# A two-layer convolution-attention kernel: image 1's first normalisation is placed amid image 0's last tiles, and the last tiles' value products are split

## The chip, the cores and the metric

The kernel runs on one core of one Trainium2 chip. Its time is device microseconds (us) of that core; a time quoted for a kernel is the median of several executions. A profile is one execution taken by the hardware profiler. Its engines are PE (TensorE, matmul), PEld (its weight loads), DVE (VectorE), ACT (ScalarE), POOL (GpSimd) and SP (SyncE, here a queue that issues DMAs).

## The reference, cut to what matters

`x` holds 2 images of 256 channels and 64 x 64 places, in float32. Two layers follow each other, each added to its input:

```python
def _gn(v, G=32, eps=1e-5):            # group normalisation over groups of 8 channels
    g = v.reshape(B_, G, C_ // G, H_, W_)
    m = jnp.mean(g, axis=(2, 3, 4), keepdims=True)
    s = jnp.var(g, axis=(2, 3, 4), keepdims=True)
    return ((g - m) / jnp.sqrt(s + eps)).reshape(v.shape)

# layer 0: attention of 8 heads of 32 channels over all 4096 places
qkv = einsum('bchw,oc->bohw', _gn(x), qkv_w) + qkv_b
attn = softmax(einsum('bhci,bhcj->bhij', q, k) * scale)
x = x + einsum('bhij,bhcj->bhci', attn, v)
# layer 1, on _gn(x): attention of 64 places inside groups, twice (first over the
# "lr" grouping, then, on its result, over the "sr" grouping), and a convolution branch
qx = relu_bn(fq2, relu_bn(fq1, feats)); kx = relu_bn(fk2, relu_bn(fk1, feats))
vx = fv(feats)
feats2 = relu_bn(srW, softmax(qx.T kx * C**-0.5) applied to vx)
x = x + rate1 * feats2 + rate2 * conv3x3(...)
```

The normalisation of an image needs its whole image: mean and variance over eight channels and 4096 places.

## The kernel before, in words

**Stages.** The images are handled one after the other. An image has 8 tiles of 512 places (`NT` = 8, `T` = 512); a tile of x is 128 partitions by 2 channel halves by 512, 512 KB. For each image the stages are: statistics and normalisation of x for layer 0 (`Stats`, lines 295 to 340; `normalise`, 366); projections to queries, keys and values (`project0`, line 416, whose results go to DRAM by line 425); the long attention (`attention0`); the first part of layer 1 (`layer1_first`); and its second part (`layer1_second`), a loop over the 8 tiles `t`.

**A tile of the second part.** It runs the q branch (two products, `fq1` and `fq2`, each followed by a relu on ACT, lines 1349, 1358 and 1137), the k branch in the same way, and `group_attention`: the scores `sp` (line 1078), values `pvs` (line 1060, two halves of two groups, each group four products on PE), a softmax (`nm`, `e`, `den`, lines 1094 to 1101: DVE, with the exponential on ACT), transposes `at` (1106), copies of them into a block-diagonal tile `bd` on DVE (1115), the product `pc` of bd and values (1124), and a relu to `res` on ACT. In between stand 16 turns of the convolution (`conv_step`): `mm`, 32 products on PE (line 996), then `z`: a copy on ACT (1001) and four sums on DVE (1002 to 1005), then additions into x (1017 to 1023). `mm` has one buffer of four PSUM banks, so the next turn's products wait for the last sum. POOL makes the transformed input `v` of a turn from the padded normalised image `xp` (982, 986). When the turns of two tiles are done, `give` (1325) adds `res` to x and SP writes it out (1331).

**Image 1's beginning.** `following` is a generator that `layer1_second` advances in image 0's last tile. It issues the loads of image 1's x (line 70) and layer 0's weights on POOL (105, 109), 16 `bn_stats` (line 321), two aggregations (325), the mean over a group's channels as a product with the matrix `group8` (328), four small operations, the variance product (337), a square root on ACT (340) and a reciprocal (341). After the second part, the loop over images allocates `xn`, the normalised image, and normalises the 16 halves of tiles into it (366). `xn` takes the one large buffer that `xp` of image 0 held.

**What sets the order.** A planner puts instructions on each engine's queue by its own estimate of their times, so an instruction written late can stand early in its queue where its inputs allow. Inside `tc.manual_schedule(engines=...)` the engines named keep the written order; in the second part this is PE alone. `tc.issue_after(kept["given"])` keeps image 1's statistics behind the last `give`. Each engine's queue is worked off in order. x has nine tile buffers (`NT + 1`): tile 0 of image 1 is loaded at the kernel's start, and each further one when a tile of image 0 has been given. The tiles `w4` of the work pool have 12 buffers; PSUM in the second part is four banks for `mm` and four more (`bank`).

Of the kernel before, what the change touches and what calls it, by code (L numbers as in the profile page):

```python
# [9 lines left out]
F32 = mybir.dt.float32  # L10
# [7 lines left out]
P = 128  # L18
B, C, H, W = 2, 256, 64, 64
N = H * W  # L20
T = 512
# [19 lines left out]
def direct_layers(ctx: ExitStack, tc: tile.TileContext, a: dict, out: bass.AP, bad: bass.AP):  # L41
# [21 lines left out]
        return psum["ps"].tile(shape, F32, tag="bank", name=name)  # L63


    def load_x(b):
        tiles = []
        for t in range(NT):
            xt = xpool.tile([P, KC, T], F32, tag="x", name=f"x_{b}_{t}")
            nc.sync.dma_start(  # L70
                out=xt,
                in_=a["x"][b, :, t * T : (t + 1) * T].rearrange("(k p) n -> p k n", p=P),
            )
            tiles.append(xt)
        return tiles
# [910 lines left out]
            (nc.gpsimd.tensor_add if plus else nc.gpsimd.tensor_sub)(dst, rows(one), rows(two))  # L986
        return v

    def conv_step(b, xts, wf, v, s, q, pacc):


        mm = pacc.tile([P, 2, 4, STRIP], F32, tag="acc", name=f"mm_{b}_{s}_{q}")
        for r in range(4):
            for m in range(2):
                for k in range(KC):
                    nc.tensor.matmul(  # L996
                        mm[:, m, r, :], wf[:, k, 4 * r + q, m * P : (m + 1) * P], v[r // 2][:, r % 2, k, :],
                        start=k == 0, stop=k == KC - 1,
                    )
        z = w4([P, 2, 2, STRIP], f"z_{b}_{s}_{q}")  # L1000
        nc.scalar.copy(z[:, 1], mm[:, :, 1, :])  # L1001
        nc.vector.tensor_add(z[:, 0], z[:, 1], mm[:, :, 0, :])  # L1002
        nc.vector.tensor_add(z[:, 0], z[:, 0], mm[:, :, 2, :])
        nc.vector.tensor_sub(z[:, 1], z[:, 1], mm[:, :, 2, :])
        nc.vector.tensor_sub(z[:, 1], z[:, 1], mm[:, :, 3, :])  # L1005
        bias = kept["bias"][1]
        for half in range(2):
            xs = xts[2 * s + half].rearrange("p m (i r j c) -> p m i r j c", i=4, r=2, c=2)
            for r in range(2):
                zs = z[:, r, :, half * (STRIP // 2) : (half + 1) * (STRIP // 2)].rearrange(  # L1010
                    "p m (i j) -> p m i j", i=4
                )
                for c in range(2):
                    dst = xs[:, :, :, r, :, c]
                    if q - c == 0:
                        for m in range(2):
                            nc.vector.scalar_tensor_tensor(  # L1017
                                dst[:, m], zs[:, m], bias[:, m, 0:1], dst[:, m], ALU.add, ALU.add
                            )
# [24 lines left out]

    SC1 = C ** -0.5

    def group_attention(nm, q, k, tokens, wv, out, busy=False, apart=False, more=None, between=None):

# [2 lines left out]

        vs = w4([P, 4, C], f"vs_{nm}")

        def values(half):
            pv = bank([P, 2, C], f"pvs_{nm}_{half}")
            for i in range(2):
                for c in range(KC):
                    nc.tensor.matmul(  # L1060
                        pv[:, i, :], tokens(c, 2 * half + i), wv[:, c, :], start=c == 0, stop=c == KC - 1
                    )
            dst = vs[:, 2 * half : 2 * half + 2, :]
            if half == 0 or busy or apart:
                nc.scalar.copy(dst, pv)
            else:
                nc.vector.tensor_copy(dst, pv)
# [20 lines left out]
            yield  # L1088
        if not first:
            values(0)  # L1090
        if not apart:
            values(1)
        nm4 = small.tile([P, 4], F32, tag="nm4", name=f"nm4_{nm}")
        nc.vector.tensor_reduce(nm4, sp, AX.X, ALU.max, negate=True)
# [22 lines left out]
            )  # L1117
        if apart:
            values(1)
        yield  # L1120
        for m in range(KC):
            pc = bank([P, T], f"pc_{nm}_{m}")
            for w in range(4):
                nc.tensor.matmul(  # L1124
                    pc[:, w * P : (w + 1) * P], vs[:, w, m * P : (m + 1) * P],
                    bd[:, w].rearrange("p a i -> p (a i)"), start=True, stop=True,
                )
            out(m, pc)
            if m == 0 and between:
                between()  # L1130

    def product(pt, wt, src, m, last=True):
        for k in range(KC):
# [145 lines left out]
    def layer1_second(b, xts, feats, mean, rstd, shift, pacc, following):  # L1279
# [28 lines left out]
        }  # L1308
        images = {1: range(5), 3: (5, 6), 4: (7,)} if b == 0 else {0: (3, 4), 1: (5,), 2: (6,), 3: (7,)}

        def conv():
            nonlocal done, wf
            if wf is None:
                wf = fetch_conv_weights(b)
            if done + 1 < len(turns):
                ahead[done + 1] = conv_transform(b, xp, *turns[done + 1])
            conv_step(b, xts, wf, ahead.pop(done), *turns[done], pacc)
            done += 1

        def give(n):  # L1320
            res = results.pop(n)
            halves = out[b, :, n * T : (n + 1) * T].rearrange("(k p) n -> p k n", p=P)
            final = b == B - 1 and n == NT - 1
            for m in range(KC):
                kept["given"] = nc.vector.scalar_tensor_tensor(
                    res[:, m, :], res[:, m, :], wts["rate1"], xts[n][:, m, :], ALU.mult, ALU.add
                )
                if final:
                    (nc.scalar if m else nc.sync).dma_start(out=halves[:, m, :], in_=res[:, m, :])
            if not final:  # L1330
                nc.sync.dma_start(out=halves, in_=res)
# [7 lines left out]
        for t in range(NT):  # L1339
# [2 lines left out]
                feats[k][:, 8 * t : 8 * t + 8].rearrange("p o d e -> p (o d e)") for k in range(KC)  # L1342
            ]

            def branch(one, two, col1, col2, nm):
                hid = w4([P, KC, T], f"h{nm}_{nt}")
                ph = [bank([P, T], f"ph{nm}_{nt}_{m}") for m in range(KC)]
                for k, m in ((0, 0), (0, 1), (1, 0), (1, 1)) if t == 0 else ((0, 0), (1, 0), (0, 1), (1, 1)):
                    nc.tensor.matmul(  # L1349
                        ph[m], wts[one][:, k, m * P : (m + 1) * P], f[k], start=k == 0, stop=k == KC - 1  # L1350
                    )
                    if k == KC - 1:
                        bn_relu(hid[:, m, :], ph[m], col1, m)
                res = w4([P, KC, T], f"r{nm}_{nt}")
                pr = [bank([P, T], f"pr{nm}_{nt}_{m}") for m in range(KC)]
                for k in range(KC):
# [5 lines left out]
                    bn_relu(res[:, m, :], pr[m], col2, m)  # L1362
                return res

            with tc.manual_schedule(engines={mybir.EngineType.PE}):
                q = branch("fq1", "fq2", V_FQ1, V_FQ2, "q")
                if pending:
                    next(pending)
# [2 lines left out]
                for tt in images.get(t, ()):  # L1371
                    to_image(tt)
                if 0 in spots.get(t, ()) and (b or t > 2):
                    conv()
                if b == 0 and t == NT - 1:
                    for n in sorted(results):
                        give(n)
                k = branch("fk1", "fk2", V_FK1, V_FK2, "k")
                if b == 0 and t == 2:
                    conv()  # L1380
                res = w4([P, KC, T], f"res_{nt}")
# [1 line left out]
                def to_res(m, pc, res=res):  # L1383
# [5 lines left out]

                parts = group_attention(  # L1390
                    nt, q, k, lambda c, w, f=f: f[c][:, w * P : (w + 1) * P], wts["fv"], to_res, apart=t + 1 < NT,
                    between=lambda: next(then) if b == 0 and t == NT - 1 else None,
                )
                next(parts)
                if 1 in spots.get(t, ()):
                    conv()
                if t < 2 and b == 0:
                    pending = parts
                else:
                    next(parts)  # L1400
                    if b == 0 and t == NT - 1:
                        next(then)
                    next(parts, None)
                    if b == 0 and t == NT - 1:
                        next(then)
                if 2 in spots.get(t, ()):
                    conv()
            if b == 0 and t == 1:
# [12 lines left out]
            results[t] = res  # L1421
            for n in sorted(n for n in results if done >= 4 * (n // 2 + 1)):
                give(n)


    ahead = {}

    def following():

        ahead.update(xts=load_x(1), w0=load_layer0(1))  # L1430
        with tc.issue_after(kept["given"].ins):
            steps = group_stats(ahead["xts"], "l0_1")
            next(steps)
        yield
        next(steps)
        yield
        ahead["stats"] = next(steps)
        yield

    for b in range(B):  # L1440
        xts = x_first if b == 0 else ahead["xts"]
        w0 = w0_first if b == 0 else ahead["w0"]
        with tc.tile_pool(name=f"ps0_{b}", bufs=8, space=PSUM) as psum["ps"]:
            mean, rstd = list(group_stats(xts, "l0_0"))[-1] if b == 0 else ahead["stats"]
            xn = apool.tile([P, KC, N], F32, tag="A", name=f"xn_{b}")
            for t in range(NT):
                for k in range(KC):
                    normalised = normalise(xn[:, k, t * T : (t + 1) * T], xts[t][:, k, :], k, mean, rstd)
# [574 lines left out]
```

## Time and profile before

| | us |
|---|---|
| median of 3 executions | 3069.78 (3066.59 to 3073.84) |
| profiled execution | 3067.66 |
| its span, first to last instruction | 3065.9 |
| mean granted clock of PE | 0.993 of full |

| stretch of the span | what runs there |
|---|---|
| 1320 to 1533 | image 0's second part, tiles 2 to 7, with the 16 convolution turns |
| 1533 to 1552 | end of tile 7, statistics of image 1 |
| 1552 to 1639 | image 1's normalisation and projections |
| 3047 to 3058 | the last tile of image 1 |

In a line of the timeline the first number is the start, the second the duration, in us from the span's start; then engine, line, operation, output and input, shapes and how many were merged; in brackets the idle time before it and what ended it. A line of the list of waits reads: who, waiting for whom: us in total, how often, longest. A table of stretches gives busy us of each engine, the granted clock of PE (1.00 is full), the mean busy share of the 16 DMA engines and the GB/s that they moved.

### The profile page before, as it was taken

To read this page: it belongs to the slowest core of one execution; us is meant where nothing else is said; L and a number is where in the kernel's file an instruction comes from. 1 tells how busy PE (TensorE), PEld (TensorE's weight loads), DVE (VectorE), ACT (ScalarE), POOL (GpSimd) and SP (SyncE) were. 2 spreads that over 40 slices of the span, in tenths; PEclk is the share of its full clock that TensorE was granted. 3 is DMA by queue.
4 is the path that set the end of the run, shared out by engine and by line. 5 is a ranking of instruction groups with operands and counts; after the bars stand their busy time and mean duration, and the time that the engine had idled before them with its cause. 6 is when DMAs were issued, how large, how long until landed. Compare 5 with 4: busy or idle time off the path is not lost. (4 is left out here: it accounts for less than half of the span.)

```text
span 3065.9 us, 63941 instructions
## 1 busy us (share of the span) xinstructions
PE 2986.3 (97%) x25129; PEld 1863.2 (61%) x25129; DVE 2456.4 (80%) x3122; ACT 2340.4 (76%) x3266; POOL 832.6 (27%) x918
## 2 busy tenths in 40 slices
PE   7999999999999999999989999999999999999998
PEld 4565566665556556677755655566555565576765
DVE  4698998989899999856556989989989999835543
ACT  2699999999999983622227999999999999734333
POOL 1122222222223240155301222322222222306440
PEclk9999999999999999999999999999999999999999
DMA  7968789787897661220159688797788976700000
GB/s 259 278 133 179 153 161 177 152 167 161 172 185 160 141 135 32 86 118 28 45 195 271 129 177 163 159 182 145 172 166 170 183 147 128 169 4 4 21 15 22
DMA packets 244148, 425.01 MB, mean 139 GB/s; under 512 B 98888, under 2 KB 109948, under 8 KB 241660
## 3 DMA queue, kind: packets, MB, share of 16 engines
q0 software_dynamic: 94720, 237.57, 40.1%
q1 hardware_dynamic: 148972, 182.99, 21.6%
q8 instruction: 199, 3.26, 0.4%
q14 instruction: 113, 0.93, 0.1%
q10 hardware_dynamic: 144, 0.26, 0.0%
HBM read 119.55 MB, written 68.39 MB: 61 GB/s over the span
## 5 line engine op out<-in xcount | busy, mean ns | idle before, releaser
L551 ACT ACTIVATE es<-ring 128x512 f32<-128x512 f32 (+2 forms) x1572 | 1203.4, 904 | 29.6 <-PE ring L545 21.7
L545 PE MATMUL ring<-q,k 128*128 128x512 f32 x4096 | 1082.3, 407 | 10.1 <-ACT v L551 4.8
L597 DVE TENSOR_TENSOR e<-e,es 128x1024 f32<-128x1024 f32 (+1 forms) x956 | 1035.3, 1144 | 23.1 <-ACT es L551 22.6
L545 PEld LDWEIGHTS ring<-q,k 128*128 128x128 f32 x4096 | 733.7, 188 | 379.8 <-ACT es L551 114.5
L551 ACT ACTIVATE v<-ring 128x512 f32<-128x512 f32 (+2 forms) x1024 | 780.7, 899 | 23.7 <-PE ring L545 12.8
L560 PE MATMUL av<-es,v 128*32 128x256 f32 (+1 forms) x9684 | 725.9, 389 | 0.0
L597 DVE TENSOR_TENSOR e<-e,v 128x1024 f32<-128x1024 f32 (+1 forms) x636 | 669.3, 1107 | 20.3 <-ACT v L551 19.3
L560 PE MATMUL av<-v 128*32 128x256 f32 (+1 forms) x6188 | 497.9, 389 | 0.0
L560 PEld LDWEIGHTS av<-es,v 128*32 128x32 f32 x9684 | 328.0, 110 | 266.1 <-issue 106.4
L560 PEld LDWEIGHTS av<-v 128*32 128x32 f32 x6188 | 221.2, 109 | 170.8 <-issue 72.4
L996 PE MATMUL mm<-v,wf 128*128 128x256 f32 x1024 | 227.6, 380 | 1.5 <-DVE z L1005 1.5
L607 POOL DMA_DIRECT2D es<-es x118 | 100.7, 853 | 465.7 <-ACT es L551 418.1
L996 PEld LDWEIGHTS mm<-v,wf 128*128 128x128 f32 x1024 | 193.3, 190 | 36.9 <-issue 9.9
L986 POOL TENSOR_TENSOR v<-col 128x512 f32<-128x512 f32 x128 | 165.4, 1319 | 177.7 <-ACT rk_sr L1137 39.3
L1001 ACT COPY z<-mm 128x512 f32<-128x512 f32 x32 | 18.7, 586 | 182.7 <-PE mm L996 182.7
L607 POOL DMA_DIRECT2D acc<-es x118 | 118.4, 1009 | 112.4 <-ACT es L551 49.3
L605 POOL DMA_DIRECT2D es<-es x20 | 11.4, 569 | 491.8 <-ACT es L551 405.6
L607 POOL DMA_DIRECT2D es<-v x72 | 61.4, 852 | 290.4 <-ACT v L551 278.0
L1002 DVE TENSOR_TENSOR z<-z,mm 128x512 f32<-128x512 f32 x32 | 22.0, 687 | 138.5 <-ACT z L1001 138.1
L607 POOL DMA_DIRECT2D v<-es x112 | 115.0, 1027 | 19.3 <-ACT es L551 11.2
L607 POOL DMA_DIRECT2D acc<-v x78 | 74.6, 957 | 78.1 <-DMA acc<-es 30.9
L982 POOL TENSOR_TENSOR col<-xp 128x1152 f32<-128x1152 f32 x32 | 69.6, 2175 | 62.1 <-DVE xp L1415 50.8
(254 smaller groups left out, 2680.0 us busy)
## 6 DMA issues: line engine op xcount, KB each, us to landing
acc<-es POOLq DMA_DIRECT2D x128, 512.0 KB, 6.4
acc<-v POOLq DMA_DIRECT2D x84, 512.0 KB, 6.2
es<-es POOLq DMA_DIRECT2D x138, 256.0 KB, 4.3
v<-es POOLq DMA_DIRECT2D x132, 256.0 KB, 5.2
k<-wk_halves SPq DMA_DIRECT2D x64, 512.0 KB
q<-wq_halves SPq DMA_DIRECT2D x256, 128.0 KB
v<-v POOLq DMA_DIRECT2D x90, 256.0 KB, 5.0
es<-v POOLq DMA_DIRECT2D x84, 256.0 KB, 3.9
```

Of the source, the lines that this page charges most:

```text
L545: touch(nc.tensor.matmul(sc[:, i, :], held["k", g // 2][:, j * P : (j + 1) * P], held["q", g, u // 2][:, u % 2, :], start=True, stop=True, ...
L551: nc.scalar.activation(dst, sc, AF.Exp, scale=SC0), set(range(at % BANKS, at % BANKS + m))
L560: note(nc.tensor.matmul(dst[HD0 * u : HD0 * u + HD0, n], lhs, rhs(u)[:, n], start=start, stop=stop))
L597: nc.vector.tensor_add(dst[:, s, :], dst[:, s, :], src)
L605: nc.gpsimd.dma_start(out=dst, in_=src)
L607: nc.gpsimd.dma_start(out=dst, in_=src, accum_op=ALU.add)
L982: (nc.gpsimd.tensor_add if plus else nc.gpsimd.tensor_sub)(col, cols(one), cols(two))
L986: (nc.gpsimd.tensor_add if plus else nc.gpsimd.tensor_sub)(dst, rows(one), rows(two))
L996: nc.tensor.matmul(mm[:, m, r, :], wf[:, k, 4 * r + q, m * P : (m + 1) * P], v[r // 2][:, r % 2, k, :], start=k == 0, stop=k == KC - 1,)
L1001: nc.scalar.copy(z[:, 1], mm[:, :, 1, :])
L1002: nc.vector.tensor_add(z[:, 0], z[:, 1], mm[:, :, 0, :])
```

## The change

Tile 7 of image 0 is called the seam: there DVE keeps the written order too, beside PE.

- `following` is advanced earlier and in smaller steps. After tile 5 it issues the loads of tiles 0 to 6 of image 1. After tile 6 it allocates image 1's `xn`, loads the last tile of x straight into its normalised place (to be normalised in place), issues the weight loads and the 16 `bn_stats`, no longer behind `give`, so that the planner may place them anywhere among tiles 3 to 6.
- In the seam tile, aggregation, mean product and spread come after the last convolution turn's products; the variance product, square root and reciprocal between the two halves of the k branch; the 16 normalisations one by one from there on: two before the scores, four behind the softmax, two behind the copies to bd, the rest around the two last products.
- `give` for tile 7 stands behind all of them on DVE.
- Tile 7 of x is loaded once more, into a tile of its own, for the addition at the end of layer 0.
- In the last tile of both images (`split`), the fourth group of values is computed behind the transposes rather than ahead of them, and the copy of the second half of values goes to ACT rather than DVE.

In the resulting queues, ACT loads the table of the square root between the relus of the k branch, and the table of the exponential again before the softmax of the seam tile; in exchange there is none at the start of image 1's attention. The `bn_stats` stand on DVE thus: tile 0 in image 0's attention; tiles 1 and 2 between e and bd of tile 3; tile 3's first half between lines 1002 and 1003 of turn 8, its second half and tile 4 behind that turn; tiles 5 and 6 around turn 12; the last tile between e and bd of tile 6. On SP, the first load of keys moves from behind the first store of values to behind the second store of queries.

```diff
-    def conv_step(b, xts, wf, v, s, q, pacc):
+    def conv_step(b, xts, wf, v, s, q, pacc, behind_products=None):
...
+        if behind_products:
+            behind_products()
         z = w4([P, 2, 2, STRIP], f"z_{b}_{s}_{q}")
...
+        pvs = {}
+
+        def values(half, places=range(2)):
+            if half not in pvs:
+                pvs[half] = bank([P, 2, C], f"pvs_{nm}_{half}")
+            pv = pvs[half]
+            for i in places:
...
+            if places[-1] == 0:
+                return
             dst = vs[:, 2 * half : 2 * half + 2, :]
-            if half == 0 or busy or apart:
+            if half == 0 or busy or apart or split:
                 nc.scalar.copy(dst, pv)
...
-        if not apart:
+        if split:
+            values(1, range(1))
+        elif not apart:
             values(1)
...
         if apart:
             values(1)
+        elif split:
+            values(1, range(1, 2))
...
             out(m, pc)
-            if m == 0 and between:
-                between()
+            if fill:
+                fill(m)
...
+            seam = b == 0 and t == NT - 1
+
+            def step(n=1):
+                for _ in range(n if seam else 0):
+                    next(then)
+
+            with tc.manual_schedule(engines={E.PE, E.DVE} if seam else {E.PE}):
...
-                    conv()
+                    conv(step)
...
-                k = branch("fk1", "fk2", V_FK1, V_FK2, "k")
+                k = branch("fk1", "fk2", V_FK1, V_FK2, "k", step)
...
+                    split=t + 1 == NT, fill=lambda m: step(3),
+                )
+                step(2)
                 next(parts)
+                step(4)
...
+            if b == 0 and t in (NT - 3, NT - 2):
+                next(then)
...
     def following():
-        ahead.update(xts=load_x(1), w0=load_layer0(1))
-        with tc.issue_after(kept["given"].ins):
-            steps = group_stats(ahead["xts"], "l0_1")
-            next(steps)
+        last_tile = slice((NT - 1) * T, N)
+        xts = ahead["xts"] = load_x(1, range(NT - 1))
         yield
-        next(steps)
+        xn = ahead["xn"] = apool.tile([P, KC, N], F32, tag="A", name="xn_1")
+        nc.sync.dma_start(out=xn[:, :, last_tile], in_=a["x"][1, :, last_tile].rearrange("(k p) n -> p k n", p=P))
+        ahead["w0"] = load_layer0(1)
+        views = [*xts, xn[:, :, last_tile]]
+        st = Stats(views, "l0_1")
+        for t in range(NT):
+            for k in range(KC):
+                st.tile(k, t)
         yield
-        ahead["stats"] = next(steps)
+        both = slice(0, KC)
+        st.aggregate(both)
+        st.means(both, bank([P, KC], "pm_l0_1"), nc.vector.tensor_copy)
+        st.spread(both)
         yield
+        pv = bank([P, KC], "pv_l0_1")
+        st.variances(both, pv)
+        st.deviations(both, pv)
+        for t in range(NT):
+            for k in range(KC):
+                yield
+                normalise(xn[:, k, t * T : (t + 1) * T], views[t][:, k, :], k, st.mean, st.rstd)
+        yield
...
-        xts = x_first if b == 0 else ahead["xts"]
+        xts = x_first if b == 0 else ahead["xts"] + load_x(1, range(NT - 1, NT))
```

More of the change, by code (lines that the diff above doesn't have):

```diff
@@ L63, in bank, with load_x @@
         return psum["ps"].tile(shape, F32, tag="bank", name=name)
-    def load_x(b):
+    def load_x(b, ts=range(NT)):
         tiles = []
-        for t in range(NT):
+        for t in ts:
             xt = xpool.tile([P, KC, T], F32, tag="x", name=f"x_{b}_{t}")
@@ L1045, in direct_layers, with group_attention @@
     SC1 = C ** -0.5
-    def group_attention(nm, q, k, tokens, wv, out, busy=False, apart=False, more=None, between=None):
+    def group_attention(nm, q, k, tokens, wv, out, busy=False, apart=False, more=None, split=False, fill=None):
         vs = w4([P, 4, C], f"vs_{nm}")
-        def values(half):
-            pv = bank([P, 2, C], f"pvs_{nm}_{half}")
-            for i in range(2):
+        pvs = {}
[4 more added lines that the diff above has]
+            for i in places:
                 for c in range(KC):
@@ L1309, in layer1_second, with conv @@
         images = {1: range(5), 3: (5, 6), 4: (7,)} if b == 0 else {0: (3, 4), 1: (5,), 2: (6,), 3: (7,)}
-        def conv():
+        def conv(behind_products=None):
             nonlocal done, wf
@@ L1316, in conv @@
                 ahead[done + 1] = conv_transform(b, xp, *turns[done + 1])
-            conv_step(b, xts, wf, ahead.pop(done), *turns[done], pacc)
+            conv_step(b, xts, wf, ahead.pop(done), *turns[done], pacc, behind_products)
             done += 1
@@ L1324, in give @@
             for m in range(KC):
-                kept["given"] = nc.vector.scalar_tensor_tensor(
+                nc.vector.scalar_tensor_tensor(
                     res[:, m, :], res[:, m, :], wts["rate1"], xts[n][:, m, :], ALU.mult, ALU.add
@@ L1343, in layer1_second, with branch @@
             ]
-            def branch(one, two, col1, col2, nm):
+            def branch(one, two, col1, col2, nm, between=None):
                 hid = w4([P, KC, T], f"h{nm}_{nt}")
@@ L1353, in branch @@
                         bn_relu(hid[:, m, :], ph[m], col1, m)
+                if between:
+                    between()
                 res = w4([P, KC, T], f"r{nm}_{nt}")
@@ L1363, in branch @@
                 return res
-            with tc.manual_schedule(engines={mybir.EngineType.PE}):
+            E = mybir.EngineType
+            seam = b == 0 and t == NT - 1
[3 more added lines that the diff above has]
+            with tc.manual_schedule(engines={E.PE, E.DVE} if seam else {E.PE}):
                 q = branch("fq1", "fq2", V_FQ1, V_FQ2, "q")
@@ L1373, in layer1_second @@
                 if 0 in spots.get(t, ()) and (b or t > 2):
-                    conv()
-                if b == 0 and t == NT - 1:
+                    conv(step)
+                if seam:
                     for n in sorted(results):
                         give(n)
-                k = branch("fk1", "fk2", V_FK1, V_FK2, "k")
+                k = branch("fk1", "fk2", V_FK1, V_FK2, "k", step)
                 if b == 0 and t == 2:
@@ L1391, in layer1_second @@
                     nt, q, k, lambda c, w, f=f: f[c][:, w * P : (w + 1) * P], wts["fv"], to_res, apart=t + 1 < NT,
-                    between=lambda: next(then) if b == 0 and t == NT - 1 else None,
+                    split=t + 1 == NT, fill=lambda m: step(3),
                 )
+                step(2)
                 next(parts)
+                step(4)
                 if 1 in spots.get(t, ()):
@@ L1400, in layer1_second @@
                     next(parts)
-                    if b == 0 and t == NT - 1:
-                        next(then)
+                    step(2)
                     next(parts, None)
-                    if b == 0 and t == NT - 1:
-                        next(then)
+                    if seam:
+                        for _ in then:
+                            pass
                 if 2 in spots.get(t, ()):
@@ L1443, in direct_layers @@
         with tc.tile_pool(name=f"ps0_{b}", bufs=8, space=PSUM) as psum["ps"]:
[L1444 to L1448, printed above, removed]
+            if b == 0:
+                mean, rstd = list(group_stats(xts, "l0_0"))[-1]
+                xn = apool.tile([P, KC, N], F32, tag="A", name="xn_0")
+                for t in range(NT):
+                    for k in range(KC):
+                        normalised = normalise(xn[:, k, t * T : (t + 1) * T], xts[t][:, k, :], k, mean, rstd)
+            else:
+                xn = ahead["xn"]
```

## The prediction

> **What bounds the kernel now.** I read the page first, then the stretch where image 0 ends and image 1 begins, then the two earlier places where the order of instructions of the changed kernel puts new vector work. The page's first line names the bound:
>
> ```profile
> PE 2986.3 (97%) x25129; PEld 1863.2 (61%) x25129; DVE 2456.4 (80%) x3122; ACT 2340.4 (76%) x3266; POOL 832.6 (27%) x918
> ```
>
> The tensor engine (PE) is busy for 97% of the span: only what opens or closes a hole on PE, or changes its clock, moves the time. The table of stretches finds the hole at the seam, 8.2 us wide and at 0.66 of the clock:
>
> ```profile
> 1520.00:1540.00 20.00, 19.31 (x98) 13.09 (x96) 12.22 (x26) 7.73 (x19) 0.00 (x0) 1.00 0.21 67
> 1540.00:1560.00 20.00, 11.77 (x34) 7.10 (x35) 16.79 (x38) 4.47 (x6) 0.00 (x0) 0.66 0.12 39
> ```
>
> (Columns: busy us of PE, PEld, DVE, ACT, POOL, then clock, DMA share, GB/s.) The list of waits in 1524 to 1560 says what PE waited for: statistics (mv), the deviation (rstd), then e and bd of the tile's softmax.
>
> ```profile
> PE p_wk L416 <- ACT rstd_l L340: 3.1, 1, 3.1
> PE pm_l L328 <- DVE mv_l L325: 3.0, 1, 3.0
> PE at_sr L1106 <- DVE e_sr L1101: 1.1, 1, 1.1
> PE pc_sr L1124 <- DVE bd L1115: 1.0, 1, 1.0
> ```
>
> In the timeline the vector engine (DVE) has 16 bn_stats (0.61 us each in a row) between 1533.3 and 1546.0, with the softmax of tile 7 among them; the first projection then runs slow:
>
> ```profile
> 1542.38 3.66 DVE L321 BATCH_NORM_STATS2 stats_l<-x 128x6 f32<-128x512 f32 x6
> 1549.99 1.28 ACT L340 ACT_TABLE_LOAD   x1
> 1551.86 7.39 DVE L366 TENSOR_SCALAR xn<-x,mean_l,rstd_l 128x512 f32<-128x512 f32 x16
> 1552.50 16.27 PE L416 MATMUL p_wk<-xn,wqk 128*128 128x512 f32 x32 [3.12 <-ACT rstd_l L340]
> 1568.61 13.90 PE L416 MATMUL p_wq<-xn,wqk 128*128 128x512 f32 x32
> ```
>
> The same 32 matmuls take 13.90 us at full clock: 2.37 us are lost to the half clock.
>
> **Part 1, the seam.** All 16 statistics leave this stretch; they go to earlier places in DVE's order (part 2). [...] I walk the new order with the old durations from the k branch's start, 1527.3.
>
> PE: the mean product, some 0.3 us, then the phk matmuls to 1531.2, the variance product 0.3, prk from 1531.5. DVE: four small operations (0.2 each) ahead of the z chain, which ends at 1532.7 instead of about 1532.0; the two res_6 of 0.7, reciprocal, xn of tile 0: free at 1535.3, before it is needed. ACT: the table load (1.28) and square root (0.26) between hk and rk, to 1533.5; three x edges (0.25 each) to 1534.25; rk0 and rk1 (0.8 each) end at 1535.9 instead of 1535.17. So the scores end at 1537.0 instead of 1536.25.
>
> Behind rk1, ACT has five small edges (1.2 us) and a second table load for the exponential, to 1538.3. This load stood at the start of image 1's attention (1638.34), hidden: PE there waited for the last value copy on DVE until 1639.11. Here it lies on the path: exp ends at 1538.8 (1538.1 before). Then den, reciprocal, product on DVE, nothing between them now, to 1539.9. PE has done 12 of the 16 value matmuls (12 x 0.233) by 1539.8: the transposes start at 1539.95 instead of 1541.02. The last four values cover to 1541.25. DVE does four normalisations (0.46 each) and only then the two bd copies (0.43 each), to 1542.6: PE waits 1.4 us. Both pc products, 1.1 each, end at 1544.85.
>
> The projection's first product waits for a scalar-engine event later than the copy that pc waited for; the only ones left are the two res_7, ending at 1545.85. So p_wk starts at 1545.95 (1544.85 if that wait is for the first). Its xn tiles are ready: the ten normalisations left end at 1547.2, p_wk takes one tile in 1.74 us. It ends at 1545.95 + 13.90 = 1559.85 instead of 1568.77: **8.9 us gained**, of which 2.4 is the clock.
>
> [...] The row is 1.28 us, and in both rows of this trace (1549.99, 1638.34) the activation behind it begins within 0.1 us of its end. [...] I take the row.
>
> The in-place tile: its load on SP waits for the last read of the padded image, the col operation that ends near 1486.9; it lands by about 1491 and is read at 1498. It passes only the two weight loads of 1517 and 1530. Nothing is paid. The first k load moves ahead of six q stores on SP; it needs the last wk store, 3.5 us older by then, and the work buffers cover more than that. The weight loads on POOL keep their place.
>
> **Part 2, where the statistics go.** Two (tile 0) go into image 0's attention: at most 1.3 us, hidden under a PE without holes; I take 0.2. Tiles 5, 6 and the in-place one fall where DVE idled 5.2 and 4.9 us; worked through, the z chain there ends at 1492.3, and PE needs it at 1495.34: nothing. Two places cost, because DVE reads a tile just after its load was issued.
>
> *Tile 3.* The new order is: z's first sum (L1002), the statistics of tile 3, then L1003, L1004, L1017, L1005. The next convolution's products (mm) have one set of banks and wait for L1005. The load stands on SP behind two result stores:
>
> ```profile
> 1428.74 4.60 SPq L1331 DMA_DIRECT2D out_dram<-res_sr  x2
> 1433.39 1.39 SPq L70 DMA_DIRECT2D x<-in_x_dram  x2
> 1432.81 0.68 DVE L1002 TENSOR_TENSOR z<-z,mm 128x512 f32<-128x512 f32 x1
> 1434.98 0.68 DVE L1005 TENSOR_TENSOR z<-z,mm 128x512 f32<-128x512 f32 x1
> 1436.97 7.07 PE L996 MATMUL mm<-v,wf 128*128 128x256 f32 x32
> ```
>
> ```profile
> 1435.00:1436.00 1.00, 1.00 (x3) 0.40 (x3) 1.00 (x4) 0.00 (x0) 0.00 (x0) 1.00 1.01 178
> 1437.00:1438.00 1.00, 1.00 (x6) 0.90 (x5) 0.50 (x2) 1.00 (x2) 0.36 (x1) 1.00 1.04 401
> ```
>
> The store of res_3 fills the engines to about 1435.6 (the dip to 178 GB/s), then 512 KB for tile 3 pass by 1437.3. At the kernel's start a tile was read 0.9 us after its bytes had passed (issued 0.73, 0.5 MB through by 3.9, read at 4.72). So DVE stands from 1433.5 to 1438.2, then 0.6 for the statistics and 2.2 to the end of L1005: 1441.1. mm starts there instead of 1436.97: **4.1 us lost**. Bounds: 3.3 if the tile counts with its last byte; 5.7 by the page's 512 KB accumulations (6.4 us from issue to landing). Behind DVE also wait an x edge with rq_5 on ACT (needed near 1456) and the v transform on POOL (needed near 1457); both are done by 1449.
>
> A PE that stands for 4 us also loses its clock. Rows: after 2.4 us idle near 1332 the clock was about half for 3.3 us; after 2.0 idle at 2307 it stayed. [...] By the rows alone it lies between 0 and 2.3. I take 1.7.
>
> *Tiles 1 and 2.* Four statistics stand between e and bd of tile 3's softmax, in 4.5 idle us. Tile 2's bytes pass by about 1375.8, so it can be read at 1376.7 and bd starts at 1378.05 instead of 1377.56; L1005, already just in time for mm there (1382.15 against 1382.29), slides with it: 0.5 lost (0 to 1.2).
>
> **Part 3, the end.** Image 1's last tile is split too: the last four value matmuls cover the transposes' copies, and the value copy (0.69) leaves DVE. e is ready at 3051.58; transposes from 3051.8 instead of 3052.56, bd to 3053.2, last value copy to 3053.75, pc done at 3055.35 instead of 3056.45: 1.1 gained (0.5 to 1.2).
>
> ```profile
> 3052.83 0.69 DVE L1067 COPY vs_sr<-pvs_sr 128x512 f32<-128x512 f32 x1 [1.25 <-PE pvs_sr L1060]
> 3054.43 2.02 PE L1124 MATMUL pc_sr<-bd,vs_sr 128*128 128x128 f32 x16 [1.49 <-DVE bd L1115]
> ```
>
> **Sum.** -8.9 - 1.1 + 4.1 + 1.7 + 0.5 + 0.2 = -3.5 us. The profiled execution took 3067.66 (span 3065.9 and 1.8 around it), so 3064.2 for its like; it lies 2.1 under the median of 3069.78, and against the median I say 3066.3.
>
> **Rivals.** *No stall at tile 3* (24%): the load is early enough, or mm doesn't need all of z. For it: mm fills its four banks one after the other and might be let in by parts. Against it: 1433.39 on SP follows a store that waits for DVE itself, and the profile's wait of mm for L1005 (1.5 us, 2 times). It gives -8.9 - 1.1 + 0.5 + 0.2 = -9.3: 3060.5. *The seam gives its gain back* (10%): the new holes of 1.4 and 1.1 us within 5 us still drop the clock (2.1 us, as p_wk lost), or the loads drain (2.5): some 3068.6. Against: the hole before the drop at 1543.6 was 1.9 of 3.4 us, the new one at most 1.5. *Slower* (8%): the wait for tile 3 on DVE outgrows the gain. Each us of later landing is one us on PE; break-even is at 3.5 us beyond my 1438.2, 8.3 us after issue instead of 4.8. Stores and loads sharing the engines could do it; the accumulations' 6.4 speaks against it. With 11 us it gives 3072.5. *The change doesn't do what it says*: excluded for the seam, since the order has mean and variance products ahead of the scores.
>
> **How the numbers follow.** 58% for my sum with its terms between their bounds: 3062.5 to 3069. The range takes in the first rival and half of the third: 3060 to 3072. A difference below 0.2%, 6.1 us, can't be told from none. Faster by more than that: most of rival one (0.20) and the edge of mine (0.12); slower by more: 0.05; the rest, 0.63, is the same.
>
> **What would show it.** Right: no bn_stats after 1527, p_wk beginning some 6 us earlier and taking about 14 us, a wait of statistics for x near 1433 to 1438 and a PE hole of some 4 us before mm there, with half clock after. Wrong: PE busy through 1441 (then rival one), p_wk still at 16 us, a hole behind the table loads above 1.3, or new holes in image 1's projections from the k load on SP.

## The result, and the profile after

| | before | after |
|---|---|---|
| median of 22 executions each, us | 3070.18 (3064.48 to 3074.26) | 3064.93 (3061.95 to 3071.46) |
| span of the profiled execution, us | 3065.9 | 3062.0 |
| mean granted clock | 0.993 | 0.994 |

The ratio is 0.9986, with a 95% interval of 0.9979 to 0.9992: 4.3 us faster (2.5 to 6.4). The forecast was 3.5 us faster and 3066.3, with "no difference above 0.2%" as the likeliest outcome; 0.14% is inside that bound.

On the page, PE's busy time hardly moves (2986.3 before), and the gain is in the holes:

```profile
PE 2987.6 (98%) x25129; PEld 1863.5 (61%) x25129; DVE 2452.9 (80%) x3120; ACT 2341.7 (76%) x3268; POOL 833.2 (27%) x918
```

**The seam.** First the table of stretches of the kernel after (columns as before: PE, PEld, DVE, ACT, POOL, clock, DMA share, GB/s), then all of PE's waits in 1524 to 1560, then its timeline at the same place:

```profile
1520.00:1540.00 20.00, 20.00 (x70) 12.59 (x69) 10.88 (x26) 8.46 (x16) 0.00 (x0) 1.00 0.08 27
1540.00:1560.00 20.00, 17.07 (x89) 10.02 (x88) 14.35 (x31) 10.43 (x21) 0.00 (x0) 1.00 0.43 147
```

```profile
PE pc_sr L1136 <- DVE bd L1125: 1.4, 1, 1.4
PE p_wk L416 <- ACT res_sr L1149: 0.9, 1, 0.9
PE sp_sr L1086 <- ACT rk_sr L1149: 0.4, 1, 0.4
PE at_sr L1116 <- DVE e_sr L1111: 0.2, 1, 0.2
```

```profile
1533.89 0.28 PE L328 MATMUL pm_l<-mv_l,group 128*128 128x2 f32 x2
1538.55 1.28 ACT L340 ACT_TABLE_LOAD   x1
1539.84 0.26 ACT L340 ACTIVATE rstd_l<-pv_l,eps 128x2 f32<-128x2 f32 x1
...
1543.32 1.28 ACT L1107 ACT_TABLE_LOAD   x1
1544.61 0.42 ACT L1107 ACTIVATE e_sr<-e_sr 128x256 f32<-128x256 f32 x1
...
1546.07 1.91 DVE L366 TENSOR_SCALAR xn<-x,mean_l,rstd_l 128x512 f32<-128x512 f32 x4
1547.89 0.85 DVE L1125 COPY bd<-at_sr 64x256 f32<-64x256 f32 x2
...
1551.78 14.00 PE L416 MATMUL p_wk<-xn,wqk 128*128 128x512 f32 x32 [0.87 <-ACT res_sr L1149]
1565.62 6.60 PE L416 MATMUL p_wq<-xn,wqk 128*128 128x512 f32 x15
```

The two waits of 3 us for statistics are gone, the clock stays at 1.00 where it was 0.66, and the first projection takes 14.00 us instead of 16.27. What is left is what the walk of the prediction had: pc waits 1.4 us for bd, which stands behind four normalisations, and the projection waits for the last relu to res (0.9; forecast 1.1). The activation behind each table load begins within 0.02 us of its end. From where the products of the last convolution turn end to the second projection PE takes 31.73 us (1533.89 to 1565.62); before it took 41.35 (1527.26 to 1568.61). So the seam gives 9.6 us.

**Turn 8.** DVE, SP and PE where the statistics of tile 3 stand between the sums:

```profile
1428.39 4.59 SPq L1343 DMA_DIRECT2D out_dram<-res_sr  x2
1433.03 1.39 SPq L70 DMA_DIRECT2D x<-in_x_dram  x2
1432.45 0.67 DVE L1004 TENSOR_TENSOR z<-z,mm 128x512 f32<-128x512 f32 x1
1437.88 0.69 DVE L321 BATCH_NORM_STATS2 stats_l<-x 128x6 f32<-128x512 f32 x1 [4.76 <-DMA x<-in_x_dram]
1439.94 0.68 DVE L1007 TENSOR_TENSOR z<-z,mm 128x512 f32<-128x512 f32 x1
1440.77 9.90 PE L996 MATMUL mm<-v,wf 128*128 128x256 f32 x32 [4.00 <-DVE z L1007]
```

DVE stands for 4.76 us until the load has landed, at 1437.88 (forecast 1438.2); the last sum (L1007) ends at 1440.6 instead of 1435.7, and PE stands for 4.00 us, begins at 1440.77 instead of 1436.97, and runs the 32 products in 9.90 us instead of 7.07. The granted clock shows it (0.50 in each slice of 1 us from 1440 to 1446):

```profile
1440.00:1460.00 20.00, 19.23 (x82) 13.33 (x84) 10.27 (x28) 6.18 (x10) 9.48 (x7) 0.84 0.00 1
```

**The end.** In the kernel after, the last values lie behind the transposes and their copy is on ACT. First two lines of before, then those of after:

```profile
3048.03 1.03 PE L1078 MATMUL sp_sr<-rk_sr,rq_sr 128*64 128x64 f32 x28 [0.52 <-ACT rk_sr L1137]
...
3058.08 0.38 ACTq L1329 DMA_DIRECT2D out_dram<-res_sr  x1
```

```profile
3046.12 1.03 PE L1086 MATMUL sp_sr<-rk_sr,rq_sr 128*64 128x64 f32 x28 [0.52 <-ACT rk_sr L1149]
...
3049.78 0.38 PE L1116 MATMUL at_sr<-ident,e_sr 128*128 128x128 f32 x2
3051.06 0.59 ACT L1073 COPY vs_sr<-pvs_sr 128x512 f32<-128x512 f32 x1 [1.36 <-PE pvs_sr L1066]
3051.20 2.10 PE L1136 MATMUL pc_sr<-bd,vs_sr 128*128 128x128 f32 x16 [0.18 <-DVE bd L1125]
3054.94 0.38 ACTq L1341 DMA_DIRECT2D out_dram<-res_sr  x1
```

From the last scores (3046.12) to the last store's issue it is 8.82 us; before it was 10.05 (3048.03 to 3058.08).

### The profile page after: what moved, and what is told of

It is laid out like the page before. It is cut to its first block, busy times and chain, and to the rows that moved or that the text cites. A ratio compares the mean times of both kernels' runs of the same rounds, so it can differ in the third digit from the quotient of the medians.

```text
span 3062.0 us, 63943 instructions
## 1 busy us (share of the span) xinstructions
PE 2987.6 (98%) x25129; PEld 1863.5 (61%) x25129; DVE 2452.9 (80%) x3120; ACT 2341.7 (76%) x3268; POOL 833.2 (27%) x918
```

## The experiments

Each is the changed kernel with one edit, but for one that starts from the kernel before and one with two edits. The theory: the seam gives 9.6 and the end 1.2 us, and the wait for tile 3's load inside turn 8 takes some 6 to 7 back, by a hole and a half clock behind it. Where a part has a rival, its expectation tells it. No run takes out the seam alone: its 9.6 us are read from the two traces, and the runs show what is left without the wait.

### Tile 3's statistics behind the sums (e_later)

```diff
-        nc.vector.tensor_sub(z[:, 1], z[:, 1], mm[:, :, 3, :])
+        kept[b, s, q] = nc.vector.tensor_sub(z[:, 1], z[:, 1], mm[:, :, 3, :])
...
-                st.tile(k, t)
+                with tc.issue_after(kept[(0, 2, 0) if t == 3 else "feats"].ins): st.tile(k, t)
```

> The changed kernel with one thing moved: the first bn_stats of tile 3 stands behind the four sums of turn 8 instead of between the first and the second. Theory (the wait for tile 3's load costs 4.2 us of hole and 2.8 us of half clock on PE): both go, so some 7 us less than the changed kernel, 11.3 less than before, ratio 0.9963; mm of turn 9 begins near 1436.6 and takes 7.07 us, and bn_stats of tiles 3 and 4 end by 1441.5, ahead of turn 9's sums near 1444.4. Rival (the stages behind turn 8 have slack that takes up the hole, and the change's 4 us are all it had to give): less than 2 us less than the changed kernel, ratio 0.998 or more.

Measured: 3059.23 against 3069.48 for the kernel before, ratio 0.9963 (0.9949 to 0.9977). The timeline of this kernel:

```profile
1436.25 0.68 DVE L1007 TENSOR_TENSOR z<-z,mm 128x512 f32<-128x512 f32 x1
1439.16 2.58 DVE L321 BATCH_NORM_STATS2 stats_l<-x 128x6 f32<-128x512 f32 x4 [0.37 <-DMA x<-in_x_dram]
1438.24 7.07 PE L996 MATMUL mm<-v,wf 128*128 128x256 f32 x32
```

The hole and the half clock are gone (the granted clock is 1.00 from 1440 to 1460; mm begins 1.27 us later than before because all of PE ahead of it does; there is no wait in front of it). The four statistics wait for the load 0.37 us and end at 1441.7, 4.3 us before the next turn's sums at 1446.0. The move is free, and 10.2 us faster than before is what the rest of the change gives, the seam and the end above all.

### The same vector work without the wait (e_same_work)

```diff
-        nc.vector.tensor_add(z[:, 0], z[:, 1], mm[:, :, 0, :])
+        kept[b, s, q] = nc.vector.tensor_add(z[:, 0], z[:, 1], mm[:, :, 0, :])
...
-                st.tile(k, t)
+                with tc.issue_after(kept[(0, 2, 0) if t == 3 else "feats"].ins): nc.vector.bn_stats(st.stats[:, k, t, :], views[2 if t == 3 else t][:, k, :])
```

> The changed kernel, with tile 2 read again in the two bn_stats of tile 3, at the same places in DVE's order; so the statistics of image 1 leave out tile 3 (tile 2 counts twice) and the output is another. It keeps the 0.6 us of vector work inside the sums and takes away the wait for the load alone. Theory (it is the wait): mm of turn 9 begins 0.6 us later than before and at full clock, 6.4 us less than the changed kernel, 10.7 less than before, ratio 0.9965. Rival (it is the vector work between the sums, whatever it reads): as the changed kernel, ratio 0.9986.

Measured: 3058.23, ratio 0.9959 (0.9945 to 0.9972). Between the sums stands a bn_stats as in the changed kernel, but of a tile long loaded:

```profile
1433.76 0.68 DVE L1465 BATCH_NORM_STATS2 stats_l<-x 128x6 f32<-128x512 f32 x1
1435.81 0.68 DVE L1007 TENSOR_TENSOR z<-z,mm 128x512 f32<-128x512 f32 x1
1437.34 7.07 PE L996 MATMUL mm<-v,wf 128*128 128x256 f32 x32
```

So it is the wait and not the work. The expectation was off by its 0.6 us: PE goes from the products before straight to mm, with no hole, since the last sum ends at 1436.5, 0.85 ahead of 1437.34. The sums have slack, and the extra 0.6 lies in it.

### The wait alone, in the kernel before (e_stall_alone)

```diff
-        nc.vector.tensor_add(z[:, 0], z[:, 1], mm[:, :, 0, :])
+        kept[b, s, q] = nc.vector.tensor_add(z[:, 0], z[:, 1], mm[:, :, 0, :])
...
         ahead.update(xts=load_x(1), w0=load_layer0(1))
+        with tc.issue_after(kept[0, 2, 0].ins): nc.vector.bn_stats(small.tile([P, 6], F32, tag="one_more", name="one_more"), ahead["xts"][3][:, 0, :])
```

> The kernel before, with one bn_stats more: of tile 3's first half of image 1, into a tile that nobody reads, between the first and the second sum of turn 8, where the changed kernel has it. Nothing else of the change is in. Theory: PE stands some 4.2 us before mm of turn 9 and then runs at half clock: 7.0 us more than before, ratio 1.0023. Rival (slack behind turn 8 takes it up): less than 2 us more, ratio 1.0006 or less.

Measured: 3075.40 against 3069.48, ratio 1.0021 (1.0011 to 1.0032): one instruction of 0.6 us costs 5.9.

```profile
1437.59 0.69 DVE L1431 BATCH_NORM_STATS2 one_more<-x 128x6 f32<-128x512 f32 x1 [4.31 <-DMA x<-in_x_dram]
1440.48 8.70 PE L996 MATMUL mm<-v,wf 128*128 128x256 f32 x32 [3.59 <-DVE z L1005]
```

The hole is 3.59 and mm takes 1.63 too long: 5.2 of the 5.9. The parts add up: 10.2 faster without the wait, 5.9 slower with nothing but the wait, and the changed kernel is 4.3 faster.

### Filling the hole (e_warm, e_warm_short)

In `conv_step`, ahead of the products of turn 9:

```diff
+        warm = bank([P, T], "warm") if (b, s, q) == (0, 2, 1) else None
+        for i in range(15 if warm is not None else 0): nc.tensor.matmul(warm, wts["fq1"][:, 0, :P], wts["fk1"].rearrange("p k c -> p (k c)"), start=True, stop=True)
```

> The changed kernel with 15 products of 128x512 put on PE ahead of turn 9's products, into a bank that nobody reads; they run in the hole that the wait for tile 3 leaves, some 3.4 of its 4.0 us. Theory (the hole halves the clock behind it): mm of turn 9 still begins near 1440.8, but takes 7.07 us instead of 9.90: 2.8 us less than the changed kernel, 7.1 less than before, ratio 0.9977. Rival (the slow products behind the hole come from something else, loads and stores for instance): mm takes 9.9 us still, and the time is that of the changed kernel, ratio 0.9986. If the 15 products don't fit, each us over is one us lost.

Measured: 3069.65, ratio 1.0000 (0.9992 to 1.0009). This missed, by a size of mine: the 15 products took 13.04 us, 0.87 each, and not 3.4. The row was there to be read (4 products of a k branch, shown as x8, take 3.60).

```profile
1437.04 13.04 PE L991 MATMUL warm<-wt_fk,wt_fq 128*128 128x512 f32 x30
1449.91 7.07 PE L996 MATMUL mm<-v,wf 128*128 128x256 f32 x32
```

mm runs at full clock (1.00 from 1440 to 1460), as the theory has it, but begins 9.1 us later than in the changed kernel. With 4 in place of 15:

> As the kernel with 15 products in the hole, with 4 of them: each took 0.87 us there, so 4 fill 3.5 of the 4.0 us. Theory (the hole halves the clock behind it): mm of turn 9 begins near 1440.8 as in the changed kernel and takes 7.07 us at full clock instead of 8.7 to 9.9: 1.6 to 2.8 us less than the changed kernel, 5.9 to 7.1 less than before, ratio 0.9977 to 0.9981. Rival (the clock was not the hole's doing): 9.9 us still, ratio 0.9986.

Measured: 3063.09 against 3069.54, ratio 0.9978 (0.9970 to 0.9985).

```profile
1438.46 3.60 PE L991 MATMUL warm<-wt_fk,wt_fq 128*128 128x512 f32 x8
1442.30 7.15 PE L996 MATMUL mm<-v,wf 128*128 128x256 f32 x32 [0.24 <-DVE z L1007]
```

DVE still waits for the load (it does nothing in the slices of 1437 and 1438 and is busy for 0.59 us of the next), but mm takes 7.15 us and the granted clock is 1.00 in each slice from 1437 to 1448. The intervals of this kernel and of the changed one overlap, so it is the rows that decide: with 0.24 us of hole left in place of 4.00, the products behind the wait ran at full clock, so their slowness goes with the hole.

### How long a hole may be (e_warm_two, e_warm_one)

The same edit with 2 products and with 1:

> As the kernel with 4 products in the hole, with 2: 1.7 of the 4.0 us are filled and a hole of some 2.3 us stays ahead of mm of turn 9. Theory (a hole needs to be longer than the 2.0 to 2.75 us after which the clock mostly stayed up elsewhere in these traces): full clock, mm takes 7.07 us, time as with 4 products, ratio 0.9978. Rival (any hole of about 2 us halves it): 8.7 to 9.9 us.

> As the kernel with 4 products in the hole, with 1: a hole of some 3.1 us stays ahead of mm of turn 9. Theory (between the 2.75 us that left the clock and the 3.6 us that halved it): half clock if its edge lies below 3.1, mm 8.7 to 9.9 us, ratio 0.9983 to 0.9986; full clock, 7.07 us, if it lies above. This run places it; neither outcome speaks against the hole as the cause.

Measured: with 2, 3062.61 against 3068.58, ratio 0.9984 (0.9976 to 0.9992); with 1, 3062.99, ratio 0.9980 (0.9971 to 0.9989). The times can't tell them apart, the rows do. First the kernel with 2, then that with 1:

```profile
1441.67 7.15 PE L996 MATMUL mm<-v,wf 128*128 128x256 f32 x32 [2.26 <-DVE z L1007]
```

```profile
1440.30 8.71 PE L996 MATMUL mm<-v,wf 128*128 128x256 f32 x32 [2.73 <-DVE z L1007]
```

A hole of 2.26 us left the clock up (1.00 in each slice from 1437 to 1451), one of 2.73 (not 3.1 as expected) halved it (0.50 in the slices of 1441 and 1442). That holds for these two executions and is no edge: in the profile of before, PE stood 2.76 us near 2770 and kept its clock, and 2.50 us near 1332 and lost it. So the expectation that a hole of 2.0 to 2.75 us mostly leaves the clock up came out here but is no rule; how these holes lay is shown in the last section.

### bd ahead of the normalisations (e_bd_first)

```diff
                 step(2)
                 next(parts)
-                step(4)
...
                     next(parts)
-                    step(2)
+                    step(6)
```

> The changed kernel with one thing moved: in the seam tile the copies to bd stand ahead of the four normalisations on DVE instead of behind them. Theory (PE's hole of 1.38 us ahead of pc is these four): bd runs from 1546.7 to 1547.6, pc waits for the second copy of values, to 1548.15, in its first half, and ends some 1.0 us earlier, and so does res_7, on which the projection waits: 1.0 us less than the changed kernel, 5.3 less than before, ratio 0.9983. Rival (then the projection waits for normalised tiles): nothing gained, ratio 0.9986. The times will hardly tell; the trace does.

Measured: 3063.45 against 3069.54, ratio 0.9983 (0.9975 to 0.9990). The planner also put the first load of keys on SP behind the last store of queries, nearer to where the kernel before had it.

```profile
1547.10 0.86 DVE L1125 COPY bd<-at_sr 64x256 f32<-64x256 f32 x2 [0.53 <-PE at_sr L1116]
1548.10 2.10 PE L1136 MATMUL pc_sr<-bd,vs_sr 128*128 128x128 f32 x16 [0.18 <-DVE bd L1125]
1551.08 5.42 PE L416 MATMUL p_wk<-xn,wqk 128*128 128x512 f32 x12 [0.87 <-ACT res_sr L1149]
```

From the scores (1542.65 here, 1542.23 in the changed kernel) to the projection it is 8.43 us instead of 9.55: 1.1 gained, and the projection still waits for the relu to res, not for a normalised tile. The hole was the four normalisations.

### The split for image 0 alone (e_split_seam)

```diff
-                    split=t + 1 == NT, fill=lambda m: step(3),
+                    split=seam, fill=lambda m: step(3),
```

> The changed kernel with the split of the last tile's values for image 0 alone; image 1's last tile computes them as before. Theory: the end is 1.2 us longer, from the transposes on (values copy on DVE ahead of bd again); 1.2 more than the changed kernel, 3.1 less than before, ratio 0.9990. Rival (the end is set by the last stores): the time of the changed kernel, ratio 0.9986. The trace has to tell, by the time from the last scores to the last store.

Measured: 3066.48 against 3069.54, ratio 0.9989 (0.9981 to 0.9997).

```profile
3045.82 1.03 PE L1086 MATMUL sp_sr<-rk_sr,rq_sr 128*64 128x64 f32 x28 [0.53 <-ACT rk_sr L1149]
...
3052.21 2.02 PE L1136 MATMUL pc_sr<-bd,vs_sr 128*128 128x128 f32 x16 [1.49 <-DVE bd L1125]
...
3055.87 0.38 ACTq L1341 DMA_DIRECT2D out_dram<-res_sr  x1
```

From the last scores to the last issue it is 10.05 us again, 1.23 more than in the changed kernel; pc waits 1.49 us for bd as it did before.

### Without the table loads (e_no_tables)

```diff
-            nc.scalar.activation(self.rstd[:, ks], pv, AF.Sqrt, bias=eps)
+            nc.scalar.activation(self.rstd[:, ks], pv, AF.Identity if self.tagn == "l0_1" else AF.Sqrt, bias=eps)
```

> The changed kernel without its two table loads in the seam tile: the square root of image 1's first statistics is replaced by a plain copy with the bias, so that image 1 is normalised with another factor and the output is another. Theory (a load costs its own 1.28 us, as its row says, and part of both lies on PE's path): scores 0.45 us earlier (PE's wait for rk goes), transposes 0.55, pc and the projection 0.85 earlier; 5.1 us less than before, ratio 0.9983. [...]

Measured: 3064.22 against 3068.58, ratio 0.9986 (0.9978 to 0.9994), the changed kernel's.

```profile
1542.99 1.03 PE L1086 MATMUL sp_sr<-rk_sr,rq_sr 128*64 128x64 f32 x28 [0.52 <-ACT rk_sr L1149]
...
1552.16 4.13 PE L416 MATMUL p_wk<-xn,wqk 128*128 128x512 f32 x9 [0.87 <-ACT res_sr L1149]
```

From the mean product (1534.60; 1533.89 in the changed kernel) to the projection it is 17.56 us instead of 17.89. Both loads together cost 0.33 us on PE's path, not 0.85. The first costs nothing: PE waits 0.52 for the second rk without it too, because that relu only begins when the last prk product is done. Of the second, 0.39 us reaches the end of the softmax on DVE.

### Both moves (e_both)

The edits of e_later and e_bd_first together.

> The changed kernel with both moves: bn_stats of tile 3 behind the sums of turn 8, and in the seam tile bd ahead of the four normalisations. Theory: the two gains add, 10.7 less than before for the first (mean of the two kernels without the wait) and 1.0 for the second: 3057.8 where before is 3069.5, ratio 0.9962. Rival: the second gives nothing, ratio 0.9965.

Measured: 3057.79 against 3069.54, ratio 0.9963 (0.9950 to 0.9975), with the stretch where the seam lies:

```profile
1540.00:1560.00 20.00, 18.96 (x58) 9.51 (x57) 14.48 (x26) 7.99 (x12) 0.00 (x0) 1.00 0.58 211
```

This is the fastest of all: 11.7 us less than the kernel before and some 7 less than the changed one. Its lead over e_later is not shown by the times; what shows the second move is e_bd_first's timeline, and its rows again here, with pc waiting 0.18 us for bd.

## Why the prediction was right, point by point

**The seam, 8.9 forecast, 9.6 in the traces.** The walk held in its order and its holes: pc waits 1.38 (1.4 forecast), the projection 0.87 for the relu to res (1.1), and the clock stays up. The sizes were a little high: the mean and variance products take 0.14 us of PE each and not 0.3, the two pc products 2.02 and not 2.2. Together with the end, the two kernels without the wait are 10.2 and 11.2 us faster than before; 10.0 was forecast for the two parts, 9.3 with the 0.7 for tiles 0 to 2. The rival in which the seam gives its gain back is out: the new holes leave the clock at 1.00. The first load of keys, which moved on SP, opens no hole: PE's waits between 1560 and 1660 are 1.6 and 0.9 us in both profiles.

**The table loads.** The row, 1.28 us, was taken as all that a load costs, and the row was right: in the profiles of the changed kernel and of e_bd_first the activation begins 0.01 to 0.02 us behind a load's end, and without both loads the projection comes 0.33 us earlier. No run shows the 2.5 us by which the loads drain in the second rival; the 0.33 us stand in their place. What the forecast had too large was their part in the path: rk was already late without a load.

**The wait for tile 3, 4.1 forecast.** It is 3.6 to 4.0 of hole in the five profiles that have it whole (4.00, 3.59, 3.74, 3.77, 3.73). The landing was forecast from the rate at which the bytes pass and came 0.3 early. The first rival (no wait; 24%) is out: the wait is there in all nine traces that have this bn_stats between the sums, and e_stall_alone has its price. So is the slower rival: the load didn't land later.

**The half clock, 1.7 forecast.** The 1.7 itself is shown by no run; the rows of before left it anywhere between 0 and 2.3. What the runs showed in its place: in the profile of after it is 2.83 (9.90 less 7.07); in the other four with the whole wait it is 1.63, 1.73, 1.67 and 1.76, and in e_warm_one 1.64. The forecast's size is the usual one, and the profile of after is the exception. A wait and its clock are thus some 5.4 us for the most part, 5.8 forecast. One row was misread on the way: the hole near 1332 is 2.50 us, not 2.4.

**Tiles 1 and 2, 0.5 forecast, 0 measured.** The four statistics run without a gap from 1374.80, and the copy to bd comes at 1377.28 (1377.56 before; the profile of after is 0.37 earlier already ahead of the change's first place):

```profile
1374.80 2.56 DVE L321 BATCH_NORM_STATS2 stats_l<-x 128x6 f32<-128x512 f32 x4 [2.46 <-DMA x<-in_x_dram]
1377.28 0.40 DVE L1125 COPY bd<-at_sr 64x256 f32<-64x256 f32 x1
```

The step that was off is the landing of tile 2, taken at 1376.7: its statistics are the third and fourth in this row and begin at 1376.1. mm of that turn begins 0.37 earlier than before (1381.92, 1382.29), so nothing is lost.

**The end, 1.1 forecast, 1.23 measured**, shown by undoing it.

**The sum.** With the sizes as the traces show them, 9.6 + 1.2 - 5.4 is 5.4; the medians give 4.3 by the ratio and 5.2 by their difference, inside an interval of 2.5 to 6.4. The forecast of 3.5 lies under them because its terms erred one way: the seam by 0.7, the wait with its clock by 0.4, tiles 1 and 2 by 0.5, the end by 0.1 (the 0.2 for tile 0 was not measured alone). What one microsecond of the measured difference is can't be settled, since the clock is lost at other places in the two profiles (at 1335.27 and 2430.94 in that of before alone, at 2306.52 and 2770.73 in that of after alone). In the profiled pair the lead is 3.0 us at 1565, 3.6 at the end of image 1's attention (2662.38 and 2658.79) and 1.9 at the last scores; between the last two nothing was changed, but the half clock lasts 10.2 us near 2662 in the profile of after against 6.8 in that of before, and 3.4 near 2770 against none.

## What to carry to other kernels

DVE took its queue in order here (it stood 4.76 us with the next sums already written behind the waiting bn_stats), so an instruction that reads a just-issued load belongs behind the last one that another engine waits for: here 0.6 us of vector work between four sums cost 5.9 us, and one ordering edge behind the sums took it back, with 4 us of idle vector time to spare. Where a planner may place work early, read the queue it made for exactly this. When a change opens a hole on PE, reckon with the half clock behind it, even if one profile doesn't show it: here it followed holes of 2.50, 2.73 and 3.59 to 4.00 us and cost mostly 1.7 us at turn 9, while a hole of 2.26 us and, in other profiles, ones of 2.50 and 2.76 left the clock up. When putting work into a hole, take its duration from a row of the same shape and type.

## What was not expected of the hardware

The same hole of PE halved the clock in one profile and not in another. In the profiles of before and after, the moments at which the granted clock changes lie whole multiples of 3.41 us apart (worked out from the granted clock in slices of 1 us). In that of before it falls at 1335.27, is back at 1338.68, falls at 1543.48 and is back at 1557.13, which is 1, 60 and 4 times 3.41 us; in that of after it falls at 1439.54, is back at 1446.36, falls at 2306.52 and is back at 2309.93: 2, 252 and 1 times.

The hole of 2.50 us near 1332 lost the clock in the profile of before and kept it in that of after; in each pair of lines first PE, then the clock (third number from the end) behind it:

```profile
1334.13 0.44 PE L1106 MATMUL at_sr<-ident,e_sr 128*128 128x128 f32 x2 [2.50 <-DVE e_sr L1101]
1335.00:1336.00 1.00, 1.00 (x5) 0.86 (x4) 0.97 (x3) 0.00 (x0) 0.00 (x0) 0.63 0.00 0
```

```profile
1335.03 0.44 PE L1116 MATMUL at_sr<-ident,e_sr 128*128 128x128 f32 x2 [2.50 <-DVE e_sr L1111]
1337.00:1338.00 1.00, 0.93 (x6) 0.66 (x6) 1.00 (x2) 0.58 (x1) 0.00 (x0) 1.00 0.00 0
```

Counted in steps of 3.41 us from the changes of each profile, 2.3 us of this hole lie in one step before, and 1.2 and 1.3 in two steps after. The hole of 2.76 us near 2770 goes the other way: 1.7 and 1.0 us in two steps before, where the clock was kept, and 2.75 in one step after, where it was lost. In e_warm_one 2.5 of the 2.73 us lie ahead of the fall at 1440.06; where the 2.26 us of e_warm_two lie is not shown, since its clock doesn't change nearby. The position doesn't sort every fall: in the 3.41 us ahead of that at 1543.48 in the profile of before PE stood 1.99 us, but 0.53 ahead of that at 113.29, and 0.7 ahead of that at 1145.99 in the profile of after, where a hole of 1.79 us from 1245.56, all in one step, left the clock up. This is sorted from traces that were there; no run moved a hole on purpose to test it.

The length of the half clock also gives the price. At turn 9 it lasts 3.40 to 3.42 us in five of the six profiles that have it, and 6.82 in that of after, where 1.2 us of the hole still lay behind the fall. At a clock of 0.50 PE loses half of what it works in that time: (6.8 - 1.2) / 2 is the 2.8 us seen there, and 1.6 to 1.8 were seen behind a half clock of 3.4 us.

And a product of 128x512 in f32 is shown by the profile as two matmuls of some 0.43 us: 15 of them, shown as x30, took 13.04 us.
